# One masked product of 2048 elements in place of two of 1024 in the second layer's attention, with new planner constants

## The chip, the cores and the metric

The kernel runs on one NeuronCore of a Trainium2 chip. The metric is the device time of one execution in microseconds; the time given for a kernel is the median of its runs. One further execution was recorded by the hardware profiler, and all views of the profile below come from that one.

## What is computed

Sixteen graphs of 1024 nodes with 256 features go through two layers. The first is a graph attention with four heads of 64, the second an attention with eight heads of 32 and a two-layer MLP. Both use the same adjacency matrix as a mask. Everything is fp32. Cut to what matters here:

```python
# layer 0, per graph: four heads; at the 0/1 adjacency only edge type 1 occurs
weight    = leaky_relu(mask * (e_src[:, None] + e_dst[None, :]))
attention = softmax(where(adj == 0, -1e9, weight))
x = layernorm(x + layernorm_per_head(relu(attention @ h + bias) + h))

# layer 1, per graph: eight heads of 32, queries = keys = values
qkv    = layernorm(x) split into 8 heads
scores = qkv @ qkv.T / sqrt(32)
attn   = softmax(where(adj > 0, scores, -inf))
x = x + attn @ qkv
x = layernorm(x + (x + gelu(layernorm(x) @ W1 + b1) @ W2 + b2))
```

## The kernel before

The kernel works through two streams of work at once. `layer0()` does the first layer of graph b+1 while `layer1()` does the second layer of graph b. Both are Python generators: each `yield` names how many units of planned work the next step is and what it waits for. A loop at the end of `fast_path` (lines 1013 to 1032) decides which of the two goes on; the choice fixes the order of instructions on PE, ACT, DVE and POOL for good, since the engines run under a manual schedule. The kernel's own `Pace` object keeps estimated times of engines and tiles for that choice; nothing of it exists on the chip.

**The second layer's attention** is `attention1` (lines 722 to 804). A step is one half of the queries (512, `HALF`), one group of four heads (`QUAD`) and one block of 128 keys (`jb`): 2 x 2 x 8 = 32 steps per graph, 512 in all. A step has three parts, and they are spread over the loop's iterations (`LAG = 3`):

- `exponentials(i)`: PE multiplies keys and queries of four heads into four PSUM banks `ps` (a ring of four), and ACT takes four exponentials of 512 elements into SBUF tiles `p`. Two heads share a tile of 128 x 2 x 512; the ring `eight` holds eight such tiles, which is four steps.
- `masked(i-1)`: DVE multiplies each of the two `p` tiles in place by the 0/1 mask (one byte per element, repeated over the two heads), 1024 elements per product.
- `products(i-3)`: PE multiplies with the values. The first two heads (`ps[0]`) are streamed against stationary values into `moved`, the other two (`ps[1]`) are loaded as weights in 32-column pieces into `held`; the first two never touch the second tile.

Between the parts, `advance()` issues pending pieces of the norm chains. The sequence on PE in one iteration is therefore: four `ps` products of step i, `moved` and `held` of step i-3; on DVE: the masks of step i-1.

**The first layer** has `prepare` (13 units per graph: transposes of x and of the mask, the projection, exponentials of its logits; PE and ACT work mostly) and `attention0` (32 steps of one unit: DVE makes two weight tiles of 512 by a max and a mask product, PE has 32 small products into `acc`). After each half of the queries a chain of norms on DVE, POOL, ACT and PE (`after0`) hands over `nT` and `v1`, from which `attention1` reads keys, queries and values of that half through `half(n)`; what isn't handed over by then is completed on the spot. The MLP of the second layer (`mlp`) follows `attention1` of each graph.

**The planner's constants** (lines 994 to 999). `WORK0` is 4 x 3.25 + 2 + 32 = 47 units for the first layer of a graph; `ATTN1` is 2 + 2.5 x 32 = 82 units for the second layer's attention, `WORK1` is 138 units with the MLP. `COURSE` says how far the first layer is wanted (in graphs) when the second is at a given unit: linear from 1.0 at the start to 1.32 at `ATTN1`, to 2.0 at 12 units before `WORK1`. `SLACK` is how far the course may be left, when the stream whose turn it is would be later than the other by more than 0.3 us; `STAY` is a hysteresis used in the MLP.

```python
which = 0 if streams[0] and (at0 < target + stay or not streams[1]) else 1
...
allowed = at0 < min(target + SLACK, place[1][0] + 2.05) if other == 0 else at0 > target - SLACK
if allowed and late[which] > max(late[other], 0.0) + 0.3:
    which = other
```

Of the kernel before, what the change touches and what calls it, by code (L numbers as in the profile page):

```python
# [31 lines left out]
F32 = mybir.dt.float32  # L32
# [3 lines left out]
AF = mybir.ActivationFunctionType  # L36
# [3 lines left out]
P = 128  # L40
# [136 lines left out]
def fast_path(  # L177
# [24 lines left out]
    nc = Pace(tc.nc)  # L202
# [6 lines left out]
    NB = N // P  # L209
    DC = D // P  # L210
    FC = DFF // P
    HALF = 512
    NH = N // HALF
    BPH = HALF // P
    Q = 32
    TILE = 64
    AHEAD = 3
    PAIR = 2
    GB = 2
    QUAD = 4  # L220
    NEAR0 = math.sqrt(0.5 - 2.0**-10)
    NEAR1 = math.sqrt(0.5 + 2.0**-10)
    SCALE1 = 1.0 / math.sqrt(HD)
# [3 lines left out]
    def ring(name, bufs, **kwargs):  # L227
        return Ring(nc, ctx.enter_context(tc.tile_pool(name=name, bufs=bufs, **kwargs)), bufs)

    one, two, three, four, eight = [  # L230
        ring(n, i) for n, i in (("one", 1), ("two", 2), ("three", 3), ("four", 4), ("eight", 8))
    ]
    small = ring("small", 3)
    memory = ctx.enter_context(tc.tile_pool(name="memory", bufs=2, space=bass.MemoryType.DRAM))
    ps_s = ring("ps_s", 4, space=PSUM)
# [40 lines left out]
    at = one.tile([P, 3, PAIR, HO, T], F32, name="v0")  # L276
# [134 lines left out]
    def when(needs):  # L411
        return max([n() if callable(n) else nc.written.get(n.tensor.name, 0.0) for n in needs] + [0.0])
# [18 lines left out]
    def begin(chain, engine, *needs):  # L431
        for n in needs:
            if not callable(n):
                uses(chain, n.tensor.name)
        chains.append([chain, engine, needs])
# [10 lines left out]
    def advance():  # L446
        for _ in range(2):
            for item in list(chains):
                if item in chains and when(item[2]) <= max(nc.now(), nc.free[item[1]]):
                    run(item)  # L450
# [271 lines left out]
    def attention1(half, mask, rinv, half_done):  # L722

        steps = [(n, quad, jb) for n in range(NH) for quad in range(H1 // QUAD) for jb in range(NB)]

        def exponentials(n, quad, jb):
            keys = slice(jb % BPH * P, (jb % BPH + 1) * P)
            of_keys, of_queries = half(jb // BPH)[2], half(n)[2]
            tiles = [ps_s.tile([P, HALF], F32, name="ps") for _ in range(QUAD)]

            nc.together(tiles)
            for e in range(QUAD):
                q = slice(e * HD, (e + 1) * HD)
                nc.tensor.matmul(tiles[e], of_keys[q, quad, keys], of_queries[q, quad, :], start=True, stop=True)
            nc.together(tiles)  # L740
            ps = []
            for e in range(0, QUAD, PAIR):
                p = eight.tile([P, PAIR, HALF], F32, name="p")
                for i in range(PAIR):
                    nc.scalar.activation(p[:, i, :], tiles[e + i], AF.Exp, scale=SCALE1)
                ps.append(p)
            return ps

        def masked(n, quad, jb, ps):
            for p in ps:  # L750
                nc.vector.tensor_mul(p, p, mask[n][:, jb, None, :].to_broadcast([P, PAIR, HALF]))

        def products(quad, jb, ps, moved, held):
            values = half(jb // BPH)[1][:, jb % BPH, :, :]
            for e in range(PAIR):
                hd = quad * QUAD + e
                for at, v in ((e, values[:, hd, 0:HD]), (PAIR + e, unit)):
                    nc.tensor.matmul(
                        moved[at * Q : (at + 1) * Q, :], v, ps[0][:, e, :], start=jb == 0, stop=jb == NB - 1
                    )  # L760
            for e in range(PAIR):
                hd = quad * QUAD + PAIR + e
                for q in range(BPH):
                    for at in range(0, P, Q):
                        nc.tensor.matmul(
                            held[at : at + Q, q, e, :],
                            ps[1][:, e, q * P + at : q * P + at + Q],
                            values[:, hd, :],
                            start=jb == 0 and e == 0 and q == 0,
                            stop=jb == NB - 1 and e == PAIR - 1 and q == BPH - 1,  # L770
                        )

        LAG = 3
        ready = {}

        def logits_ready():
            return ps_s.ready("ps", QUAD)

        def outs_ready():
            return ps_o.ready("po", 2)  # L780

        for i in range(len(steps) + LAG):
            if i < len(steps):
                ready[i] = exponentials(*steps[i])
                advance()
            if 0 <= i - 1 < len(steps):
                masked(*steps[i - 1], ready[i - 1])
                advance()
            if i < LAG:
                yield 1.0, logits_ready  # L790
                continue
            n, quad, jb = steps[i - LAG]
            if jb == 0:
                moved = ps_o.tile([P, HALF], F32, name="po")
                held = ps_o.tile([P, BPH, PAIR, HD + 1], F32, name="po")
            products(quad, jb, ready.pop(i - LAG), moved, held)
            if jb == NB - 1:
                if quad == 0:
                    o = one.tile([P, BPH, D], F32, name="o0")
                chain = heads_out(n, quad, moved, held, o, rinv)  # L800
                begin(chain, "vector", held, moved, o)
                if quad == H1 // QUAD - 1:
                    half_done(n, o, chain)
            yield (2.5, logits_ready, *ready.get(i - LAG + 1, ()), *([outs_ready] if jb == NB - 1 else []))

    def heads_out(n, quad, moved, held, o, rinv):

        oT = two.tile([P, HALF], F32, name="oT1")
        nc.scalar.copy(oT, moved)
        of_heads = o.rearrange("p k (h e) -> p k h e", e=HD)  # L810
        rinv = rinv[:, n * BPH : (n + 1) * BPH, :]

        def divide(first, sums, src):
            heads = slice(quad * QUAD + first, quad * QUAD + first + PAIR)
            nc.vector.reciprocal(rinv[:, :, heads], sums)
            nc.vector.tensor_mul(
                of_heads[:, :, heads, :], src, rinv[:, :, heads][:, :, :, None].to_broadcast([P, BPH, PAIR, HD])
            )

        yield "vector", held  # L820
        divide(PAIR, held[:, :, :, HD], held[:, :, :, 0:HD])
        yield "tensor", oT, side_ready
        pt = side_bank([P, BPH, QUAD, Q])
        for q in range(BPH):
            nc.tensor.transpose(
                pt[:, q, :, :].rearrange("p e z -> p (e z)"), oT[:, q * P : (q + 1) * P], ident
            )
        yield "vector", pt
        divide(0, pt[:, :, PAIR:, 0], pt[:, :, 0:PAIR, :])
# [164 lines left out]
    WORK0 = NB // GB * 3.25 + 2.0 + NB * H0 * 1.0  # L994
    ATTN1 = 2.0 + 2.5 * (NH * NB * H1 // QUAD)
    WORK1 = ATTN1 + NB // GB * (1.75 * FC / 2 + 3.5 * GB)
    SLACK = 0.083
    STAY = 0.017
    COURSE = [(0.0, 1.0), (ATTN1, 1.32), (WORK1 - 12.0, 2.0), (WORK1, 2.0)]

    def wanted():
        b, done = place[1]
        for (start, low), (end, high) in zip(COURSE, COURSE[1:]):
            if done < end:
                return b + low + (high - low) * (done - start) / (end - start)
        return b + COURSE[-1][1]

# [5 lines left out]
    streams, needs, which = [layer0(), layer1()], [(), ()], 0  # L1013
    while any(streams):
        (b0, done0), target = place[0], wanted()
        at0 = b0 + done0 / WORK0

        stay = 0.0 if place[1][1] < ATTN1 else (STAY if which == 0 else -STAY)
        which = 0 if streams[0] and (at0 < target + stay or not streams[1]) else 1
        if all(streams):  # L1020
            late = [when(n) - nc.now() for n in needs]
            other = 1 - which
            allowed = at0 < min(target + SLACK, place[1][0] + 2.05) if other == 0 else at0 > target - SLACK
            if allowed and late[which] > max(late[other], 0.0) + 0.3:
                which = other
        step = next(streams[which], None)
        if step is None:
            streams[which], needs[which] = None, ()
        else:
            place[which][1] += step[0]  # L1030
            needs[which] = step[1:]
        advance()
# [447 lines left out]
```

## Time and profile before

| | us |
|---|---|
| median of three runs | 3459.49 |
| the three runs | 3459.29, 3459.49, 3473.02 |
| the profiled execution | 3472.71 |
| span of the profile (first to last instruction) | 3470.9 |
| PE busy | 3321.2 (96%) |
| DVE busy | 2982.8 (86%) |
| ACT busy | 1937.3 (56%) |
| POOL busy | 418.9 (12%) |

The span is 1.8 us shorter than the profiled execution's own time, and that execution was 13.2 us longer than the median. PE's busy time is the union of its matmuls, whose ends are modelled: a matmul that waits in the middle of a group can still count as busy, so 96% isn't 96% of the array's peak. All instructions that go through the kernel's recording helper carry the same line, L61, so groups are told apart by the names of their tiles (`p<-p,mask` is the masked product, `p<-ps` the exponential, `p<-cb,dinv,mask` a weight tile of the first layer). A graph takes some 211 us once both streams run.

### The profile page before, as it was taken

The page shows a single profiled execution, that of the slowest core. Times are in us where ns is not written, and L with a number is a line of the kernel's source. Part 1 is how long each engine was busy: PE and PEld are TensorE (multiplying, and loading weights), DVE is VectorE, ACT ScalarE, POOL GpSimd, SP SyncE. Part 2 cuts the span into 40 slices and gives each one's busy share as a digit, 9 for nine tenths or more (in the row PEclk, how much of TensorE's full clock was granted, in tenths as well). Part 3 has the DMA queues.
Part 4 walks back from the last instruction along what each step waited for, and adds up shares of the span by engine and source line. Part 5 has one row for each costly group of instructions (what it writes and reads, how often), then busy time and mean ns, then how long its engine had stood idle before and what let it go on. Part 6 is the DMA issues. An engine that isn't in the chain of part 4 may idle for free.

```text
span 3470.9 us, 141029 instructions
## 1 busy us (share of the span) xinstructions
PE 3321.2 (96%) x64161; PEld 2259.7 (65%) x64161; DVE 2982.8 (86%) x5262; ACT 1937.3 (56%) x4192; POOL 418.9 (12%) x424
## 2 busy tenths in 40 slices
PE   5799999999999999999999999999999999999998
PEld 5458576675856758576585766757667585765846
DVE  5898898988979898898988989889898888989873
ACT  2563846547375573745638466473655737466363
POOL 1102011010110101101020110101101011010200
PEclk9899999999999999999999999999999999999999
DMA  5211202011020111202112020120201112020000
GB/s 135 50 22 37 47 25 58 15 44 40 28 59 21 41 34 33 56 18 58 23 35 48 24 57 18 41 43 27 60 20 40 37 31 59 20 54 10 26 3 14
DMA packets 95727, 131.30 MB, mean 38 GB/s; under 512 B 10384, under 2 KB 61584, under 8 KB 95120
## 3 DMA queue, kind: packets, MB, share of 16 engines
q1 hardware_dynamic: 75104, 87.58, 8.2%
q0 software_dynamic: 18432, 33.56, 6.7%
q8 instruction: 504, 8.26, 1.0%
q10 hardware_dynamic: 1584, 1.05, 0.1%
q14 instruction: 103, 0.84, 0.1%
HBM read 138.68 MB, written 17.04 MB: 45 GB/s over the span
## 4 chain that ended last, share of the span: by engine, by line
PE 72%; DVE 20%; ACT 5%; issue 2%; DMA 0%; POOL 0%; ACTq 0%; POOLq 0%; DVEq 0%
PE po L61 28%; PE ps L61 25%; PE acc L61 19%; DVE p L61 15%; ACT p L61 2%; DVE o L61 1%; DVE x L61 1%; ACT sq L61 1%; DVE st L61 1%; DVE z L61 1%; ACT mask L61 1%; ACT hb L61 1%; DMA w0e<-in_L_gnn_W_dram 0%; DVE v L61 0%; ACT z L61 0%
## 5 line engine op out<-in xcount | busy, mean ns | idle before, releaser
L61 ACT ACTIVATE p<-ps 128x512 f32<-128x512 f32 x2048 | 1061.9, 615 | 403.5 <-PE ps L61 374.8
L61 DVE TENSOR_TENSOR p<-p,mask 128x1024 f32<-128x1024 f32 x1024 | 1187.4, 1219 | 11.9 <-ACT p L61 11.9
L61 DVE SCALAR_TENSOR_TENSOR p<-cb,dinv,mask 128x512 f32<-128x512 f32 x1024 | 711.7, 746 | 0.1
L61 PE MATMUL ps<-nT 32*128 32x512 f32 x4096 | 687.1, 655 | 2.2 <-ACT p L61 2.2
L61 ACT ACTIVATE hid<-ps,b_sb 128x256 f32<-128x256 f32 x512 | 242.6, 474 | 794.9 <-PE ps L61 793.7
L61 PEld LDWEIGHTS po<-v,p 128*32 128x32 f32 x32768 | 395.5, 110 | 335.3 <-issue 287.1
L61 PE MATMUL acc<-v,p 128*64 128x65 f32 x16384 | 563.1, 227 | 33.6 <-DVE p L61 15.8
L61 PEld LDWEIGHTS acc<-v,p 128*64 128x64 f32 x16384 | 517.0, 140 | 114.4 <-issue 55.6
L61 PE MATMUL po<-p,v 128*32 128x512 f32 x2048 | 553.6, 616 | 0.0
L61 PE MATMUL po<-p,unit 128*32 128x512 f32 x2048 | 553.1, 615 | 0.0
L61 PE MATMUL ps<-yT,w_sb 128*128 128x256 f32 x2048 | 489.8, 385 | 0.0
L61 PE MATMUL po<-w_sb,hid 128*128 128x256 f32 x2048 | 474.6, 384 | 0.0
L61 PEld LDWEIGHTS po<-w_sb,hid 128*128 128x128 f32 x2048 | 382.1, 190 | 54.0
L61 PEld LDWEIGHTS ps<-yT,w_sb 128*128 128x128 f32 x2048 | 376.0, 190 | 51.1
L61 PE MATMUL po<-v,p 128*32 128x33 f32 x32768 | 391.1, 198 | 13.5 <-issue 9.6
L61 PEld LDWEIGHTS ps<-nT 32*128 32x128 f32 x4096 | 227.3, 187 | 104.9 <-issue 41.7
L61 PEld LDWEIGHTS po<-p,v 128*32 128x32 f32 x2048 | 78.6, 109 | 332.1 <-issue 174.6
L61 POOL TENSOR_TENSOR r<-v,mhalf 128x1 f32<-128x1 f32 (+1 forms) x192 | 157.9, 831 | 706.4 <-DVE v L61 624.5
L61 DVE TENSOR_TENSOR z<-acc,bias_r 128x256 f32<-128x256 f32 x128 | 54.2, 424 | 183.5 <-ACT hb L61 183.3
L61 PE MATMUL acc<-w0e,xT 128*128 128x264 f32 x512 | 152.1, 421 | 38.4 <-DVE z L61 23.0
L61 POOL DMA_DIRECT2D ak<-in_adj_dram x128 | 69.7, 545 | 974.6 <-PE acc L61 962.0
L61 POOL TENSOR_TENSOR r<-v1s,mhalf 128x4 f32<-128x4 f32 x32 | 61.5, 1923 | 992.0 <-DVE v1s L61 992.0
(108 smaller groups left out, 2745.6 us busy)
## 6 DMA issues: line engine op xcount, KB each, us to landing
ak<-in_adj_dram POOLq DMA_DIRECT2D x128, 256.0 KB, 3.9
cb<-esr SPq DMA_DIRECT2D x64, 512.0 KB
xk<-in_x_dram SPq DMA_DIRECT2D x64, 256.0 KB
xl<-in_x_dram SPq DMA_DIRECT2D x32, 512.0 KB
out_dram<-z SPq DMA_DIRECT2D x128, 128.0 KB
w_sb<-in_L_gnn_W_dram SPq DMA_DIRECT2D x2, 1024.0 KB
esr<-rows SPq DMA_DIRECT2D x64, 4.0 KB
v<-in_L_gnn_a_src_dram SPq DMA_DIRECT2D x2, 320.0 KB
```

The costliest lines, as they stand in the source:

```text
L61: return method(*args, **kwargs)
```

## The change

The exponentials of all four heads of a step go to one tile `p` of 128 x 4 x 512 in the ring `four` (four steps again, the same bytes), `masked` multiplies the whole tile with one product of 2048 elements, and `products` reads heads 0 and 1 for `moved` and heads 2 and 3 for `held` from that tile. The ring `eight` is gone. Five constants of the planner change with it: `SLACK` from 0.083 to 0.065, `STAY` from 0.017 to 0.013, the course from 1.32 to 1.41 at the end of the attention and its end from 12 to 10 units before the end of the MLP, and the lateness at which the other stream is preferred from 0.3 to 0.5 us.

```diff
-    one, two, three, four, eight = [
-        ring(n, i) for n, i in (("one", 1), ("two", 2), ("three", 3), ("four", 4), ("eight", 8))
-    ]
+    one, two, three, four = [ring(n, i) for n, i in (("one", 1), ("two", 2), ("three", 3), ("four", 4))]
...
-            ps = []
-            for e in range(0, QUAD, PAIR):
-                p = eight.tile([P, PAIR, HALF], F32, name="p")
-                for i in range(PAIR):
-                    nc.scalar.activation(p[:, i, :], tiles[e + i], AF.Exp, scale=SCALE1)
-                ps.append(p)
-            return ps
-
-        def masked(n, quad, jb, ps):
-            for p in ps:
-                nc.vector.tensor_mul(p, p, mask[n][:, jb, None, :].to_broadcast([P, PAIR, HALF]))
-
-        def products(quad, jb, ps, moved, held):
+            p = four.tile([P, QUAD, HALF], F32, name="p")
+            for e in range(QUAD):
+                nc.scalar.activation(p[:, e, :], tiles[e], AF.Exp, scale=SCALE1)
+            return p
+
+        def masked(n, quad, jb, p):
+            nc.vector.tensor_mul(p, p, mask[n][:, jb, None, :].to_broadcast([P, QUAD, HALF]))
+
+        def products(quad, jb, p, moved, held):
...
-                        moved[at * Q : (at + 1) * Q, :], v, ps[0][:, e, :], start=jb == 0, stop=jb == NB - 1
+                        moved[at * Q : (at + 1) * Q, :], v, p[:, e, :], start=jb == 0, stop=jb == NB - 1
...
-                            ps[1][:, e, q * P + at : q * P + at + Q],
+                            p[:, PAIR + e, q * P + at : q * P + at + Q],
...
-    SLACK = 0.083
-    STAY = 0.017
-    COURSE = [(0.0, 1.0), (ATTN1, 1.32), (WORK1 - 12.0, 2.0), (WORK1, 2.0)]
+    SLACK = 0.065
+    STAY = 0.013
+    COURSE = [(0.0, 1.0), (ATTN1, 1.41), (WORK1 - 10.0, 2.0), (WORK1, 2.0)]
...
-            if allowed and late[which] > max(late[other], 0.0) + 0.3:
+            if allowed and late[which] > max(late[other], 0.0) + 0.5:
```

## The prediction

> **What bounds the kernel now.** I read the page's shares first, then its chain of what ended last, then one graph in four windows, then single groups. The page:
>
> ```profile
> PE 3321.2 (96%) x64161; PEld 2259.7 (65%) x64161; DVE 2982.8 (86%) x5262; ACT 1937.3 (56%) x4192; POOL 418.9 (12%) x424
> PE 72%; DVE 20%; ACT 5%; issue 2%; DMA 0%; POOL 0%; ACTq 0%; POOLq 0%; DVEq 0%
> PE po L61 28%; PE ps L61 25%; PE acc L61 19%; DVE p L61 15%; ACT p L61 2%; DVE o L61 1%; DVE x L61 1%; ACT sq L61 1%; DVE st L61 1%; DVE z L61 1%; ACT mask L61 1%; ACT hb L61 1%; DMA w0e<-in_L_gnn_W_dram 0%; DVE v L61 0%; ACT z L61 0%
> ```
>
> PE sets the end for most of the span, but DVE's `p` products, both layers', hold 15% of the chain, some 520 us. The windows of one graph (columns: length; busy and count for PE, its weight loads, DVE, ACT, POOL; PE clock; DMA share; GB/s) show where:
>
> ```profile
> 1391.00:1411.00 20.00, 16.95 (x144) 9.34 (x142) 17.59 (x46) 14.75 (x37) 3.61 (x5) 0.85 0.22 54
> 1411.00:1456.00 45.00, 44.92 (x1116) 23.64 (x1115) 34.90 (x41) 37.49 (x85) 2.63 (x5) 0.99 0.34 72
> 1456.00:1512.00 56.00, 53.50 (x1446) 29.02 (x1446) 54.12 (x74) 37.37 (x80) 2.46 (x2) 1.00 0.06 9
> 1512.00:1602.00 90.00, 90.00 (x1314) 77.41 (x1311) 78.67 (x169) 31.34 (x62) 17.36 (x14) 1.00 0.13 34
> ```
>
> The **start** of a graph (first line) waits for the norm chain, PE idles 3 us and its clock falls to 0.85. The **middle** of the attention is PE's, with 10 us of DVE idle. Its **tail** (steps 18 to 31) has DVE at 97%. The MLP stretch is PE's without a hole. How the tail looks on each engine, by the timelines:
>
> ```profile
> 1487.55 6.89 DVE L61 TENSOR_TENSOR p<-p,mask 128x1024 f32<-128x1024 f32 x6
> 1494.94 1.41 DVE L61 SCALAR_TENSOR_TENSOR p<-cb,dinv,mask 128x512 f32<-128x512 f32 x2
> ```
>
> ```profile
> 1456.65 1.14 PE L61 MATMUL ps<-nT 32*128 32x512 f32 x8
> ```
>
> Six masked products stand in 6.89 us, so one follows the other every (6.89 - 1.22)/5 = 1.134 us, though one lasts 1.219: ends overlap. An undisturbed `ps` group takes 1.07 to its successor (1.14 with its own end). Where two attention steps follow without first-layer work, it stretches to 1.4 to 1.8, as its PSUM banks are still being read by the exponentials. In the tail of this graph these stretches are 1.10 (step 18), 0.52 (22), 0.74 (23), 1.14 (25) and 1.10 us (30): 4.6 us per graph.
>
> The group lines of the page:
>
> ```profile
> L61 ACT ACTIVATE p<-ps 128x512 f32<-128x512 f32 x2048 | 1061.9, 615 | 403.5 <-PE ps L61 374.8
> L61 DVE TENSOR_TENSOR p<-p,mask 128x1024 f32<-128x1024 f32 x1024 | 1187.4, 1219 | 11.9 <-ACT p L61 11.9
> L61 DVE SCALAR_TENSOR_TENSOR p<-cb,dinv,mask 128x512 f32<-128x512 f32 x1024 | 711.7, 746 | 0.1
> ```
>
> The masked product waits for exponentials only 11.9 us in all: DVE comes to it late, with the work ready.
>
> **What the Trainium skill says.** "VectorE: DVE Perf Modes", section "The TRN2 errata", gives an fp32 tensor_tensor of N elements (N + 151)/0.96 ns; at 1024 that is 1224, and the trace has 1219. The same section says that the SBUF latency is paid between instructions, once for a large tile and once for each small one. "Perfetto Trace Analysis", section "Optimizing Scalar/DVE Operations", names about 60 ns of it as engine time, the rest overlapping the next instruction; the trace agrees: 1134 - 1024/0.96 = 67 ns. The section also says that where DVE isn't saturated but makes bubbles elsewhere, breaking instructions up lets work complete sooner: the cost of this change in one sentence. "TensorE: Matmul & The Clock Gate", Part 1, says that idle stretches halve PE's clock; `po<-p,v` groups at 1.06 instead of 0.59 us in the start agree.
>
> **The change, part by part.**
>
> *The product.* 512 steps lose one instruction. No row has 2048 elements. By the skill's form the product lasts (2048 + 151)/0.96 = 2291 ns, and the next starts 85 ns before its end, as now: 2.20 us against 2 x 1.134 = 2.268. Bounds: 2048/0.96 = 2.133 below, 2.268 (nothing saved) above. I take 0.067 us. DVE loses 512 x 0.067 = 34.3 us of work. It reaches the end only where DVE sets it: about 11 saturated steps (21 to 31) per graph, 11 x 0.067 = 0.74 us, times 16 graphs = **-11.8 us** (bounds 0 and 2 x 11.8 = -23.6). Elsewhere DVE's idle time swallows it.
>
> *The added wait, on ACT.* The first product needed two exponentials; the whole one needs four, 1.03 us later. Pairing each first product with its step's fourth exponential in the trace, 60 of 512 steps have it start earlier, 40.7 us in sum. Behind it on DVE wait the projection's `z` and `v` (which free PSUM for PE) and the norms. These are steps in which DVE has caught up, so its idle 10 us in the middle of each graph cover this (40.7/16 = 2.5 us per graph); with the cover gone, all 40.7 us.
>
> *The added wait, on PE.* `moved` needed the first half only; now it needs the end of the whole product. Moving the end to the later of start and fourth exponential plus 2.29 us, `moved` would start too early in 33 steps (up to three per graph, among steps 23, 30 and 31), 14.0 us in sum; elsewhere the two steps between mask and products hide it (median slack 4.0 us). `held` behind it waited for the second product anyway, and the `ps` products of the next step are queued behind both. I take **+14.0**; bounds 0 (if `held`'s present wait absorbs it) and 14.0 plus the 40.7 above.
>
> *Buffers.* Four tiles of four heads hold the same four steps as eight of two. A tile is free after `held` instead of `moved`, but the exponentials that reuse it follow `ps` products that PE issues after `held`: 0. The exponentials, DMAs and matmuls stay the same in number; nothing passes SP's queue or POOL's: 0.
>
> *The planner.* Of 47 units of first layer, the course wants 0.32 x 47 = 15.0 by the attention's end now, 18.9 with the slack, and 0.41 x 47 = 19.3 then, 22.3 with the slack. The trace has 6 `attention0` steps there, 14 + 6 = 20 units: it rides the upper limit. A lateness of 0.5 us asked for where 0.3 was enough will invoke the slack less often. So 0 to 3 more first-layer steps come into the tail. Each brings 2 x 0.662 = 1.32 us of DVE (start to start), and 1.08 us of PE, which leaves the MLP stretch: at DVE's bound 0.24 us each is lost, 0 to 0.7 us per graph; each also fills a stretched `ps` group, worth up to 1.1. I can't price the order better from the trace, and take **0**, with the rivals as ends.
>
> Sum against the profiled execution: 3472.7 - 11.8 + 14.0 = 3474.9. It ran 13.2 above the median, so for the median 3459.5 + 2.2 = **3462**.
>
> **Rivals.**
>
> *The order gets better (faster).* If the added steps fill the stretched groups: at half of 4.6 us per graph, over 15 graphs, -34.5, so 3425; with all of the product's 11.8 as well and no late `moved`, 3413. For it: all stretches lie where no first-layer work stands between. Against: DVE is full there, so a filled hole may become a wait for DVE.
>
> *The start of a graph gets worse (slower).* The course ends 2 units later in the MLP: by 8 matmuls of 0.216 us for 1.75 units, 2.0 us. From the last `acc` product of `attention0` to the start of the attention are 9.65 us, and `nT` of the second half is complete 13.9 us after it; step 4, the first to need it, starts at 15.5 us in five graphs and later in the others, at about 18 in most. The margin is 1.6 us in the first kind. A shift of 2.0 costs from 0.4 us; with PE at half clock while it waits and the norm pieces completed on the spot, up to 3 us per graph: +6 to +45, so 3468 to 3507 with the sum above. It decides once `nT` comes later than about 15.5 us. Against: the lower course in the MLP needs fewer first-layer steps there (0.59 x 47 = 28 instead of 32).
>
> *The change doesn't do what it says:* a product of 2048 followed every 2.268 us. Then 3459.5 + 14.0 = 3473, still the middle case.
>
> **How the numbers follow.** A difference of 0.5% (17 us) is about what a measurement of this kernel can tell from none. Little change, 3444 to 3477: 0.42, the likeliest, hence 3462. The better order, below 3442: 0.22. Slower, the late start or waiting DVE: 0.36, as both added waits and the later end of the first layer's course point that way, and DVE has no room in the tail for more steps. The range goes from 3418, most of the better order, to 3507, the end of the late start.
>
> **What would show it.** Right: `p<-p,mask` x512 at about 2290 ns, DVE's busy time down by about 34 us, a wait on ACT `p` grown from 11.9 to at most 50 us, six to nine `acc<-v,p` groups before the MLP. Better order: `ps` groups of 1.07 throughout the tail. Late start: a longer stretch with PE's clock under 0.9 at each graph's start. Wrong altogether: PE's busy time itself changed by more than the span, or ACT's `p` waiting for free tiles.

## The result, and the profile after

The changed kernel takes 3494.95 us (median of five runs, 3492.6 to 3497.17) against 3463.56 us of the kernel before in the same series. The ratio is 1.0087, with a 95% interval of 1.0066 to 1.0107: slower by 30 us. The time lies inside the stated range, but not in the case that the prediction called the likeliest.

The busy times on the page of the changed kernel:

```profile
PE 3353.8 (96%) x64161; PEld 2293.9 (66%) x64161; DVE 2947.9 (84%) x4750; ACT 1934.7 (55%) x4192; POOL 420.9 (12%) x424
```

DVE's busy time fell by 34.9 us, as 512 dropped instructions should make it. PE's *rose* by 32.6 us with the same 64161 matmuls, and the span by 22.3. The page's groups say where:

```profile
L61 ACT ACTIVATE p<-ps 128x512 f32<-128x512 f32 x2048 | 1063.4, 618 | 463.1 <-PE ps L61 462.6
L61 DVE TENSOR_TENSOR p<-p,mask 128x2048 f32<-128x2048 f32 x512 | 1156.8, 2284 | 46.3 <-ACT p L61 46.2
L61 PE MATMUL ps<-nT 32*128 32x512 f32 x4096 | 733.2, 651 | 3.4 <-ACT p L61 2.5
L61 PE MATMUL po<-p,v 128*32 128x512 f32 x2048 | 555.6, 618 | 18.9 <-DVE p L61 18.9
```

The same two PE groups in the kernel before:

```profile
L61 PE MATMUL ps<-nT 32*128 32x512 f32 x4096 | 687.1, 655 | 2.2 <-ACT p L61 2.2
L61 PE MATMUL po<-p,v 128*32 128x512 f32 x2048 | 553.6, 616 | 0.0
```

The 46 us more of `ps<-nT` are no work: a group that waits for a PSUM bank in its middle counts as busy throughout. One can see it in the timeline of PE after the first norm of a graph, `po` lines left out (start, length, engine, instruction):

```profile
1417.54 1.14 PE L61 MATMUL ps<-nT 32*128 32x512 f32 x8
...
1420.17 1.77 PE L61 MATMUL ps<-nT 32*128 32x512 f32 x8
...
1423.42 1.14 PE L61 MATMUL ps<-nT 32*128 32x512 f32 x8
...
1426.06 1.76 PE L61 MATMUL ps<-nT 32*128 32x512 f32 x8
```

The same place in the kernel before has first-layer work (`acc`) between the attention steps:

```profile
1414.18 0.62 PE L61 MATMUL acc<-identb,ak 128*128 128x128 bf16 x8
1414.73 1.23 PE L61 MATMUL ps<-nT 32*128 32x512 f32 x8
...
1417.44 1.16 PE L61 MATMUL acc<-w0e,xT 128*128 128x264 f32 x4
1418.53 1.14 PE L61 MATMUL ps<-nT 32*128 32x512 f32 x8
...
1421.16 0.62 PE L61 MATMUL acc<-identb,ak 128*128 128x128 bf16 x8
1421.71 1.21 PE L61 MATMUL ps<-nT 32*128 32x512 f32 x8
```

I call an attention step *bare* if nothing but its own value products (`po`) stands between its `ps` group and the next. A normal graph has 5 bare steps before and 10 after (103 and 176 in all). The step's own matmuls take 2.63 us; of two bare steps in a row the second takes 3.25. ACT's timeline in the first three of these steps of the changed kernel shows why:

```profile
1418.70 2.06 ACT L61 ACTIVATE p<-ps 128x512 f32<-128x512 f32 x4 [0.45 <-PE ps L61]
1421.33 2.07 ACT L61 ACTIVATE p<-ps 128x512 f32<-128x512 f32 x4 [0.56 <-PE ps L61]
1424.58 2.06 ACT L61 ACTIVATE p<-ps 128x512 f32<-128x512 f32 x4 [1.19 <-PE ps L61]
```

The four exponentials begin when the whole `ps` group is done and take 2.06 us. The first four end at 1420.76, but the next `ps` group starts at 1420.17 and needs the same four banks, so its last products wait. ACT isn't late here: it stands idle before each of these steps and waits for PE.

The windows of one graph of the changed kernel, cut at its own steps 4, 18 and the MLP (columns as in the prediction):

```profile
1397.00:1417.00 20.00, 16.88 (x144) 9.76 (x143) 17.39 (x42) 14.66 (x36) 4.04 (x5) 0.84 0.22 53
1417.00:1465.00 48.00, 48.00 (x1185) 25.51 (x1185) 35.83 (x29) 37.33 (x85) 2.12 (x4) 1.00 0.28 58
1465.00:1522.00 57.00, 56.76 (x1496) 33.13 (x1494) 55.24 (x64) 37.39 (x80) 3.03 (x3) 1.00 0.13 27
1522.00:1610.00 88.00, 86.86 (x1190) 74.39 (x1191) 75.25 (x164) 31.42 (x62) 16.71 (x14) 1.00 0.11 29
```

The start is as it was. PE has no hole in the middle, though it does less first-layer work there. In means over 14 graphs, in us, from the starts of steps 0, 4 and 18 and the end of the last value product (the last column is the kernel of experiment e1 below):

| stretch | before | after | one product, old order |
|---|---|---|---|
| start, steps 0 to 3 | 17.3 | 17.0 | 16.5 |
| middle, steps 4 to 17 | 48.1 | 47.4 | 48.1 |
| tail, steps 18 to 31 | 56.4 | 61.7 | 56.0 |
| MLP, to the next graph | 88.7 | 85.7 | 88.7 |
| graph | 210.5 | 211.8 | 209.2 |

First-layer work that the middle didn't take came into the tail, and three `attention0` steps came there from the MLP. The MLP gave back 3 us for them; the tail took 5.3.

### The profile page after: what moved, and what is told of

Read it like the earlier page. It is cut to its first block, busy times and chain, and to the rows that moved or that the text cites. A ratio compares the mean times of both kernels' runs of the same rounds, so it can differ in the third digit from the quotient of the medians.

```text
span 3493.2 us, 140001 instructions
## 1 busy us (share of the span) xinstructions
PE 3353.8 (96%) x64161; PEld 2293.9 (66%) x64161; DVE 2947.9 (84%) x4750; ACT 1934.7 (55%) x4192; POOL 420.9 (12%) x424
## 4 chain that ended last, share of the span: by engine, by line
PE 73%; DVE 18%; ACT 6%; issue 2%; DMA 0%; POOL 0%; ACTq 0%; POOLq 0%; DVEq 0%
PE po L61 29%; PE ps L61 27%; PE acc L61 17%; DVE p L61 16%; ACT p L61 2%; ACT mask L61 1%; ACT sq L61 1%; ACT o L61 1%; DVE z L61 0%; DVE x L61 0%; ACT z L61 0%; DMA w0e<-in_L_gnn_W_dram 0%; ACT hb L61 0%; DVE o L61 0%; DVE hb L61 0%
## 5 line engine op out<-in xcount | busy, mean ns | idle before, releaser
L61 DVE TENSOR_TENSOR p<-p,mask 128x2048 f32<-128x2048 f32 x512 | 1156.8, 2284 | 46.3 <-ACT p L61 46.2
L61 PE MATMUL ps<-nT 32*128 32x512 f32 x4096 | 733.2, 651 | 3.4 <-ACT p L61 2.5
L61 PE MATMUL po<-p,v 128*32 128x512 f32 x2048 | 555.6, 618 | 18.9 <-DVE p L61 18.9
L61 PE MATMUL ps<-yT,w_sb 128*128 128x256 f32 x2048 | 476.8, 383 | 0.0
L61 PEld LDWEIGHTS ps<-nT 32*128 32x128 f32 x4096 | 259.5, 185 | 117.9 <-ACT p L61 52.4
```

Source lines behind the costliest of these rows:

```text
L61: return method(*args, **kwargs)
```

## The experiments

All ratios are to the kernel before, in interleaved runs on the same chip; e1 to e4, e5 to e8, e9 to e11 and e12 ran on four different chips. Since line numbers differ between the kernels, groups are again named by their tiles.

**e1 and e2: product and order taken apart.** In e1 the product is whole, but the planner is told what it was told before, so that every engine has the old order. The diff, against the changed kernel, is cut to the mask and one constant.

```diff
-            nc.vector.tensor_mul(p, p, mask[n][:, jb, None, :].to_broadcast([P, QUAD, HALF]))
+            for h in halves:
+                nc.enter("vector", "tensor_mul", (h, h, mask[n][:, jb, :]), {})
+            nc.nc.vector.tensor_mul(p, p, mask[n][:, jb, None, :].to_broadcast([P, QUAD, HALF]))
...
-    SLACK = 0.065
+    SLACK = 0.083
...
```

> One masked product of 2048 in one tile of four heads, with the old constants, and with the planner told of two products: PE, ACT, POOL, SP and DVE have the old order, instruction by instruction, except that each two products of the mask are one. Order theory (the loss lies in where first-layer steps stand between attention steps; 103 attention steps of 512 have nothing between them and the next, as in the kernel before): ratio to before 0.997 to 1.003. Product theory (the loss is the later start and end of the whole product): 1.006 to 1.010, near 3492 us. By the prediction's own sum: +2.2 us, 1.0006; moved waits for the masked product at step 31 by 0.7 to 1.0 us per graph.

Measured: 3447.44 us, 0.996 (0.9946 to 0.9973). The product alone is a **gain** of 0.4%, with 1 outside the interval, and just below the range of the order theory.

e2 is its mirror: the changed kernel's order with two products.

```diff
-            nc.vector.tensor_mul(p, p, mask[n][:, jb, None, :].to_broadcast([P, QUAD, HALF]))
+            seen = mask[n][:, jb, None, :]
+            nc.enter("vector", "tensor_mul", (p, p, seen.to_broadcast([P, QUAD, HALF])), {})
+            for e in range(0, QUAD, PAIR):
+                pair = p[:, e : e + PAIR, :]
+                nc.nc.vector.tensor_mul(pair, pair, seen.to_broadcast([P, PAIR, HALF]))
```

> The changed kernel's order (all five new constants, one tile of four heads, planner told of one product) with the mask in two products of 1024 again. The mirror of the run before. Order theory: near the changed kernel, ratio to before 1.006 to 1.011, ps<-nT busy near 733 us as in the changed kernel (687 before), 176 bare attention steps. Product theory: back to 0.997 to 1.003.

Measured: 3491.45 us, 1.0092 (1.0078 to 1.0107), as slow as the changed kernel. Their `ps<-nT` groups, of e1 and then of e2:

```profile
L75 PE MATMUL ps<-nT 32*128 32x512 f32 x4096 | 685.1, 654 | 2.5 <-ACT p L761 2.5
```

```profile
L61 PE MATMUL ps<-nT 32*128 32x512 f32 x4096 | 734.5, 653 | 2.3 <-ACT p L61 1.5 <-issue 0.8
```

685 with one product, 734 with two: the stretching goes with the order, not with the product. Product theory falls, order theory stands. In the new order the whole product doesn't show its gain (1.0087 and 1.0092 can't be told apart).

**e5 and e6: what in the order.** If the stretched groups wait for banks that exponentials read, shorter exponentials must take the difference between the orders away. Both kernels get the same edit, which leaves out half of each exponential (cut; the mask's product also becomes a maximum of the same size):

```diff
-                nc.scalar.activation(p[:, e, :], tiles[e], AF.Exp, scale=SCALE1)
+                nc.nc.scalar.activation(p[:, e, 0 : HALF // 2], tiles[e][:, 0 : HALF // 2], AF.Exp, scale=SCALE1)
```

> One whole product, the old order (as in the first run), but each exponential does 256 of its 512 elements; the rest of p keeps the value 1 from the start, and the mask product is a maximum of the same size, so that values stay finite (the attention's result is left out by this). PSUM banks are freed earlier, everything else stands where it was. With the same edit in the changed kernel's order beside it: release theory (the 47 us between 3447 and 3495 are ps products waiting for banks that exponentials still read) expects both at about the same time, within 12 us of each other, and this one at 3360 to 3420, as its own bare steps lose their wait too (ps<-nT to next PE start 694 us now, 550 without any wait).

> The changed kernel with each exponential at 256 of its 512 elements, otherwise as the run before (same stand-in values, mask product a maximum). Release theory: within 12 us of the run before, down from 47. Rival (the new order costs by DVE's queue in the tail, or by array switching, not by PSUM banks): still 35 to 60 us slower than it.

Measured: 3379.38 us (0.977, 0.9742 to 0.9797) in the old order, 3369.43 us (0.9739, 0.9712 to 0.9767) in the new. The 47 us between the orders are gone; the new one is even 10 us ahead. The exponentials' groups of e5 and e6, in this order:

```profile
L763 ACT ACTIVATE p<-ps 128x256 f32<-128x256 f32 x2048 | 621.3, 395 | 524.2 <-PE ps L75 496.0 <-issue 28.1
```

```profile
L744 ACT ACTIVATE p<-ps 128x256 f32<-128x256 f32 x2048 | 623.5, 398 | 636.9 <-PE ps L61 636.4
```

The `ps<-nT` groups are busy 593.5 us in e5 and 601.5 us in e6, 8 us apart where 48 lay between the orders. So the new order's loss passes through the time that exponentials take. By the stretches of the table above, the middle of a graph falls from 47.4 to 44.8 us in the new order and only from 48.1 to 47.5 in the old: the new order's middle has less work, and the waits for banks had hidden it. Not all of the gain is this: a graph's start falls by over 3 us in both orders. The edit frees ACT as a whole, not the banks alone, so by itself it doesn't separate a late bank from a late ACT queue; for the bare steps of the middle, ACT's idle time in the timeline above does.

**e3, e4 and e7: which constant.** The lateness threshold is the constant that makes bare steps, so I put it back alone (e3), and put it alone into the kernel before (e4).

```diff
-            if allowed and late[which] > max(late[other], 0.0) + 0.5:
+            if allowed and late[which] > max(late[other], 0.0) + 0.3:
```

> The changed kernel with one constant back: the other stream is preferred from 0.3 us of lateness again, not 0.5. In its order 56 of 512 attention steps are bare (103 before, 176 in the changed kernel); 7 first-layer attention steps stand in the attention phase of a graph as in the changed kernel (4 before). Lateness theory (the threshold alone makes bare steps, each some 0.43 us, 31.4 us/73): 56 - 103 = -47 steps, -20 us, ratio 0.992 to 0.997. Course theory (the steeper course overfills the tail, where DVE is full): it stays at 1.006 to 1.010.

> The kernel before with only the lateness threshold at 0.5 us: 222 bare attention steps against 103 before. Lateness theory at 0.43 us for a bare step: +51 us, ratio 1.012 to 1.018, more than the whole change cost. Course theory: no change, 0.997 to 1.003.

Measured: e3 3538.79 us, 1.0222 (1.0208 to 1.0236); e4 3543.4 us, 1.0236 (1.0215 to 1.0257). Both lie outside the ranges named for them. e4 goes the way of the lateness theory, and further: with 222 bare steps it lost 83 us. e3 refutes that theory as the whole story: with 56 bare steps, as few as any kernel here has, it lost 78 us. The timelines of e3 in a graph's tail, DVE first, then PE:

```profile
1497.86 1.22 DVE L61 TENSOR_TENSOR o<-o,x 128x1024 f32<-128x1024 f32 x1
...
1501.45 1.22 DVE L61 TENSOR_TENSOR x<-x,o 128x1024 f32<-128x1024 f32 x1
1502.58 2.29 DVE L61 TENSOR_TENSOR p<-p,mask 128x2048 f32<-128x2048 f32 x1
```

```profile
1499.55 1.75 PE L61 MATMUL ps<-nT 32*128 32x512 f32 x8
1504.92 1.06 PE L61 MATMUL po<-p,v 128*32 128x512 f32 x1 [3.63 <-DVE p L61]
```

The masked product stands behind a norm of 4.7 us (from `o<-o,x` to the start of the mask) on a DVE that is late already. PE idles 3.63 us for it, and then runs at half clock, as the windows of e3 around it show in the third column from the end:

```profile
1490.00:1500.00 10.00, 10.00 (x279) 5.53 (x279) 9.86 (x17) 6.78 (x14) 0.00 (x0) 1.00 0.02 5
1500.00:1504.00 4.00, 1.30 (x8) 0.29 (x2) 3.86 (x9) 2.19 (x5) 1.94 (x1) 0.87 0.02 4
1504.00:1510.00 6.00, 5.08 (x84) 2.60 (x84) 6.00 (x6) 2.66 (x5) 0.00 (x0) 0.52 0.01 3
```

e7 asks whether the whole product is to blame for that: two products with the new course.

```diff
-    SLACK = 0.083
-    STAY = 0.017
-    COURSE = [(0.0, 1.0), (ATTN1, 1.32), (WORK1 - 12.0, 2.0), (WORK1, 2.0)]
+    SLACK = 0.065
+    STAY = 0.013
+    COURSE = [(0.0, 1.0), (ATTN1, 1.41), (WORK1 - 10.0, 2.0), (WORK1, 2.0)]
```

> The kernel before (two products, lateness 0.3) with SLACK, STAY and COURSE of the changed kernel. Beside the run with the whole product and the same four constants (3538.8, which loses 5 us per graph where the masked product stands behind a norm on DVE while PE waits). 71 bare steps. If that loss is the steeper course's: 1.018 to 1.026. If it is the whole product's later end (moved could have begun 1.1 us earlier, keeping PE's clock up): 0.995 to 1.008.

Measured: 3530.35 us, 1.021 (1.0185 to 1.0234). The steeper course loses nearly as much with two products. So each half of the new constants costs some 2% by itself and both together 0.9%. The orders show a difference that fits. In e3 preparation is done by step 18, and `attention0` steps, which need DVE, stand from step 20 on, ahead of the norm. In the changed kernel the higher threshold has moved preparation from the middle into steps 18 to 23, and `attention0` steps stand only from step 25 on, after the norm. That this is what makes the two halves milder together wasn't tried by itself.

PE's clock goes with it. In the tail of a graph the half clock is granted for 4.4 us in e3, 2.9 in e4 and 3.9 in e7 (means over 14 graphs), and not at all in the kernel before and the changed one. As half of that time is lost at most, I estimate up to 33, 22 and 29 us over 15 graphs, so up to between a quarter and two fifths of these losses can be clock and not bare steps.

**e8 to e11: is there a better order?** e8 ends the course earlier, for the wait at a graph's start.

```diff
-    COURSE = [(0.0, 1.0), (ATTN1, 1.32), (WORK1 - 12.0, 2.0), (WORK1, 2.0)]
+    COURSE = [(0.0, 1.0), (ATTN1, 1.32), (WORK1 - 26.0, 2.0), (WORK1, 2.0)]
```

> One whole product, planner told of two as in the first run, old constants but the course ends 26 units before the MLP's end, not 12: the first layer's last norm chain finishes in the MLP and its transposes stand there. It is meant to take the wait at a graph's start away (steps 1 to 3, some 5 to 8 us per graph). If the start's wait is that chain: 3380 to 3430. If DVE, now also given the first layer's work faster in the MLP, becomes the bound there: 3447 to 3500.

Measured: 3460.25 us, 0.9998 (0.9983 to 1.0013). The start shrinks (steps 0 to 3 take 13.9 us, 15.5 to 18.3 in the kernel before), but PE's idle time before first-layer products that wait for DVE's weights rises from 16.7 us (e1) to 41.9, and the MLP stretch from 88.7 us (e1) to 92.2: the gain is given back, and e8 is 13 us slower than e1.

e9 and e10 let masked products pass between the pieces of the norm, in the order of e3 and of e1; e11 is e10 with the course's end at 20 units.

```diff
         for g in range(BPH):
+            yield "vector", o
             statistics(o[:, g, :], mv[:, g, :])
+        yield "vector", mv
...
+        yield "vector", o
         nc.vector.tensor_add(x1, x1, o)
```

> As the run e3 (the changed kernel with lateness 0.3, 3538.8), but the norm after the attention (finish1) gives way between its pieces: a yield on DVE before each of its four statistics and before the addition of x1, so that a masked product can stand between them. In its DVE order a masked product now stands before the statistics, where 5.7 us of norm stood in one piece. If that piece was the cause of the 3.6 us wait on PE at step 22 and the half clock after it, some 5 us per graph: 3440 to 3480. If DVE is short of time as a whole in this tail: 3510 to 3545.

> As the first run (one whole product, old constants, planner told of two, 3447.4), with the norm of finish1 in pieces. 88 bare steps, 103 there. At 0.43 us a bare step: -6 us, 3441; if the order of the norm costs elsewhere (its end comes later and the MLP waits): 3447 to 3465.

> As the run before, and the course ends 20 units before the MLP's end (26 units took the wait at the start away and gave it back in the MLP: 3460). If the start's wait shrinks before DVE becomes the MLP's bound: 3400 to 3435. If both move together: 3441 to 3460.

Measured: e9 3549.97 us, 1.0261 (1.0233 to 1.0288); e10 3462.29 us, 1.0009 (0.9999 to 1.002); e11 3464.14 us, 1.0019 (1.0009 to 1.0028). None helps: e9 is no faster than e3, and e10 and e11 are some 15 us slower than e1; e9 and e11 lie 4 to 5 us above the ranges named for them. In e9 the wait partly moved. Its waits on PE (us, times, longest):

```profile
PE acc L61 <- DVE relu L61: 54.7, 16, 6.1
PE po L61 <- DVE p L61: 45.9, 15, 3.1
```

Fifteen late masked products again, one per graph (54.3 us in e3), and now sixteen waits for a reader of an `acc` bank (6 and 12.9 us in e3). This fits a DVE that is short of time as a whole in a tail that takes the steeper course's work, where what stands first in its queue only decides who waits; no run shows it by itself.

**e12: the product as one would write it.** One product, old constants, and the planner counts one product. Against e1, cut to the mask:

```diff
-            for h in halves:
-                nc.enter("vector", "tensor_mul", (h, h, mask[n][:, jb, :]), {})
-            nc.nc.vector.tensor_mul(p, p, mask[n][:, jb, None, :].to_broadcast([P, QUAD, HALF]))
+            nc.vector.tensor_mul(p, p, mask[n][:, jb, None, :].to_broadcast([P, QUAD, HALF]))
```

> The product part of the change as it would be written: one tile of four heads, one product of 2048, old constants, and the planner counts it as one product, so the order shifts a little (PE first differs from the kernel before in the first graphs; 103 bare steps as there, at steps 17, 24, 25, 27 and 29 of a graph). If the gain of the first run (0.996) is the product's and not that of the exact old order: 0.994 to 0.998. If the order decides: anything from 0.994 to 1.005.

Measured: 3476.32 us, 1.004 (1.0022 to 1.0057). Same instructions and constants as e1, 0.8% slower, and slower than the kernel before too: the gain of e1 comes only with its exact order. What differs in a normal graph looks small: the transposes after the norm stand in step 22, not 23, a step 27 is bare in place of a 22, and `moved` of step 23 waits 0.7 us for its mask. The stretches don't put the loss there: the tail takes 56.1 us (56.0 in e1), but the start 17.1 (16.5) and the MLP 89.0 (88.7). e1, with the old order kept by hand, is the fastest kernel that does the whole work here.

## Why the prediction was right or wrong

**The product's own time: right.** It lasts 2284 ns (2291 by the form that the prediction took from the Trainium skill, "VectorE: DVE Perf Modes", section "The TRN2 errata"), and one follows another in 2.20 us (e1 and after): the 0.067 us saved per step are there, as are the 34 us of DVE.

**The path's share of it, -11.8: right as a number, in part by luck.** e1 gained 12.8 us by the medians. But its stretches put only 0.4 us per graph in the tail, not 0.74, and 0.8 in the start, where the prediction had none. The start comes mostly in two lengths, as these two graphs of e1 show (the third column from the end is PE's clock):

```profile
755.80:774.10 18.30, 15.26 (x135) 8.00 (x134) 15.90 (x41) 14.89 (x37) 3.61 (x5) 0.83 0.25 58
966.50:982.00 15.50, 13.70 (x135) 7.00 (x134) 13.16 (x35) 14.35 (x37) 3.60 (x5) 0.89 0.29 70
```

In the long one the half clock is granted for 6.8 us (its last 0.6 us behind the window), in the short one for 3.4. Of the 15 starts after the first graph, 9 are short in e1's profiled execution, and 5 in those of the kernel before, the changed kernel and e2. Four such graphs at 2.8 us are 11 of the 20 us between the profiled executions of e1 and the kernel before. Why e1 has more short starts is not shown.

**The wait on ACT: right.** It grew from 11.9 to 46.3 us in after (44.6 in e1), under the 50 named, and it didn't show in the time: e1 gains all the same.

**The wait on PE, +14.0: wrong in size.** In the old order e1 shows 2.4 us of it. The pairing left each product's start where it was. But in the saturated tail every earlier product also ends sooner: at step 23 the mask starts 10.60 us after its `ps` group in e1 and 10.87 before (medians over 11 graphs). `moved` starts 0.06 us after the product's end at steps 23 and 31: just in time. In the new order the wait is there, 18.9 us in the changed kernel, at steps 30 and 31 of each graph. But little of it is the whole product's: with two products in that order (e2) `moved` waits 8.7 us, and `held` starts 0.25 us late behind it. Taken together, PE waits 1.38 us in these two steps with one product and 1.23 with two. So 0 was the better of the two bounds, and the sum would have been -11.8, a small gain at the edge of what can be told.

**The planner, taken as 0: wrong, and this decided.** The step counted well (zero to three more first-layer attention steps; six became nine before the MLP) and named the very effect, stretched `ps` groups. It erred twice. It read the lateness threshold only in the tail: asking for 0.5 us also removes first-layer work from steps 4 to 9, in the middle, which I had called PE's without asking what stands between its steps. And it let stretched groups stand as a gain to be had, 4.6 us per graph, not as a loss that could double. The order is worth (1.0092 - 1) x 3460 = 32 us with two products (e2), and with one 44 us by the ratios (1.0087 - 0.996) or 47 by the medians (3494.95 - 3447.44).

**The rivals.** The late start fell: `nT` of the second half is complete 13.87 us after the start (13.89 before) and the last `acc` product stands 9.65 us ahead of it in both. The better order did not come. "Slower" was right by 0.36 for a reason that the text named under another head. That 3494.95 lies in the range is luck in that sense: the range reaches so far, to 3507, for the late start, and the late start didn't come.

**A sign that I had wrong.** I wrote that PE's busy time changing by more than the span would show the account wrong altogether. It did change by more (32.6 and 22.3), and the account was wrong in its planner step, but not altogether. The sign was too wide: waits inside a group count as busy, so any order that stretches more groups sets it off.

**What stays open.** I took 31 us over 73 bare steps, 0.43 us each, as a price. It doesn't carry: e4 pays more (83 us for 119, clock included), e3 loses with fewer, and e10 gains nothing by them. Bare steps, DVE's backlog and PE's clock act together, and no count that I made before a run predicted the order's time. What costs e12 its 29 us to e1 was not taken apart. Nor was SLACK or STAY tried by itself.

## What to carry to other kernels

When a change comes with new constants of a planner that fixes the order, cost the order as carefully as the instruction: here the new product gained 0.4% in the old order and lost 0.4% when planned anew, and the new constants lost over 1%. Test them apart by keeping the old order, instruction by instruction, under the new product. In a stretch where two engines are both full, shift work into it only after adding up both engines' time there; a group of matmuls that waits for PSUM in its middle hides its wait in PE's busy time, so compare the same group's busy time between kernels.

## What the runs showed of the hardware that I had not expected

An idle PE costs twice. After 3.63 us of waiting in e3 the granted clock stood at 0.52 over the next 6 us, and `po<-p,v` groups lasted 1.06 us where they last 0.59 to 0.62, so that step took 9.2 us for some 3.2 us of its own matmuls. An order that makes one such wait per graph can lose more than the wait: e3 waits 54.3 us in all for late masked products, and lost 78.

A graph's start in e1 takes 15.5 us where the half clock is granted for 3.4 us of it and some 18.3 where it is granted for 6.8, with the same instructions. A difference of 0.4% between two kernels can lie in how often each comes, so count them before giving a cause.
